# A two-layer graph network with an expert-choice FFN: gathers of 128 rows, a written order of the engines, and a + relu(b − a) on TensorE

## The chip, the cores and the metric

The program runs on one NeuronCore of a Trainium2 chip. A core has five engines with their own instruction streams: TensorE (PE, matmuls, with a separate stream of weight loads, PEld), VectorE (DVE), ScalarE (ACT), GpSimd (POOL) and SyncE (SP), and 16 DMA engines that all of them share. An engine takes its instructions strictly in the order in which they stand in its stream; engines wait for each other through semaphores. The metric is the time of one execution on the device in microseconds. Three runs of the kernel before took 1171.47, 1177.69 and 1181.61 us; the median, 1177.69 us, is what the changed kernel is compared with.

## The reference

The input is a matrix `x` of 1250 nodes with 512 features, and a list of 41,250 edges sorted by destination. All data are fp32.

```
def graph_conv_max(x, src, dst, W_rel, b, W_root):
    agg = segment_max(x[src], dst, num_segments=1250)
    agg = where(isfinite(agg), agg, 0)
    return agg @ W_rel.T + b + x @ W_root.T

h = relu(graph_conv_max(layernorm(x), ..., W1_rel, b1, W1_root))
h = relu(graph_conv_max(h,            ..., W2_rel, b2, W2_root))
x = x + h
y = layernorm(x)                       # 1250 x 512
# expert choice: 8 experts, each takes the 512 nodes with the highest probability
probs = softmax(y @ Wr, axis=0)
x = x + sum over experts of  prob * (gelu(y[chosen] @ W1 + b1) @ W2 + b2)
```

A node has 33 incoming edges on average, so a layer takes the maximum over some 41,250 rows of 2 KB.

## The kernel before

The nodes lie in ten tiles of 125 (`TN`, `NT`). The rows that may be sources stand in DRAM in `table_d`, ten blocks of 126 rows: 125 nodes and one row of −1e30. The same rows are in SBUF as `xb`. The function `fast_gnn` does the two graph layers, `expert_choice` the rest; a slower general version behind a flag is not run for these inputs. The maximum for a tile of 125 destinations is put together from three kinds of sources:

- **Blocks** (`from_blocks`, line 380 for the matmuls). For each destination tile and each of the ten source blocks, up to two sources per destination are picked by a one-hot matrix: two fp32 matmuls, (126 x 125 one-hot)ᵀ times (126 x 512 of `xb`), into the two halves of a PSUM tile `pq`. ACT first casts the one-hots from bf16 to fp32 (`ohf`, line 376), two blocks at a time. DVE takes the maximum of the whole `pq` (125 x 1024) into `acc2` (lines 386 and 388), and at the end of a tile joins the two halves. That is 200 matmuls and 90 such maxima in a layer.
- **Own gathers.** Seven more sources per destination (`K0`, indices `nat_i`) are fetched from `table_d` by indirect DMAs on POOL's queue. One such gather brings one row for each of the 125 destinations.
- **Late gathers.** What is left over is written to `rest_d` in an order sorted by how much is left (indirect DMAs, line 347), read back as dense lists `late_i`, gathered (107 gathers in a layer), and the maxima are stored to `ovf_d`. Each node fetches its row from there by its `slot_i`.

In `fetched` (line 402), up to four gathers fill one of the four buffers `hb` (pool `hist`), and DVE reduces them (lines 406 to 417). In `aggregate`, a tile whose sources are all in is transposed on PE, multiplied by `W_rel`, and added to the root part `x @ W_root + b`, which `root_part` (lines 222 to 248) has stored to `root_d` earlier. In the first layer `hidden` writes the result to `xb` and `table_d[1]`; in the second `residual` adds `x`, normalizes, stores `y_d` and transposes it into `yT`.

Ahead of the first layer stands a prefix. It finds for each node where its edges begin (`q_f`, ten gathers `row_i` at line 168, `first`), fetches each node's 64 keys (`win`, line 194), and a loop over the ten tiles (lines 259 to 298) then sorts each node's sources into blocks, own and rest: some 30 short DVE instructions for each tile (`cand`, `top`, `sel`, `new`, `ov`). From the block lists PE and ACT make a small tile `lt`, which goes through DRAM (`idx_d`) and comes back spread over 126 partitions as `ohs`.

Nothing in `fast_gnn` fixes the order of the instructions: a scheduler lays each engine's stream from its own estimates, and so interleaves, for instance, the DVE instructions of two tiles, or puts all ten root parts of the second layer (PE, 525 to 580 us) ahead of its blocks.

Of the kernel before, what the change touches and what calls it, by code (L numbers as in the profile page):

```python
# [20 lines left out]
NEGT = -1.0e30  # L21

def fast_gnn(tc, ctx, sh, io, y_d):
# [26 lines left out]
    keep = ctx.enter_context(tc.tile_pool(name="fkeep", bufs=1))  # L52
    key_d = dram.tile([1, NE + W], F32, name="key_d")
# [4 lines left out]
    ovf_d = dram.tile([N, D], F32, name="ovf_d")  # L58
# [15 lines left out]

    fr_i = gw.tile([1, NF], I32, name="fr_i")
# [5 lines left out]
    df, jle, key = (scratch[:, k * LE:(k + 1) * LE] for k in range(3, 6))  # L81
    nc.sync.dma_start(d_i, dst)
    nc.scalar.dma_start(s_i, src)
    pl_i = gw.tile([P, 1], I32, name="pl_i")
    nc.vector.memset(pl_i, 0)
# [3 lines left out]
    for t in range(NT):  # L89
        (nc.scalar if t % 2 else nc.sync).dma_start(acc[:TN, t, :], x[t * TN:(t + 1) * TN, :])  # L90

    node = gw.tile([P, NT], F32, name="node")
    nc.gpsimd.iota(node, pattern=[[TN, NT]], base=0, channel_multiplier=1,
                   allow_small_or_imprecise_dtypes=True)
    iota_w = gw.tile([P, W], F32, name="iota_w")
    nc.gpsimd.iota(iota_w, pattern=[[1, W]], base=0, channel_multiplier=0,
                   allow_small_or_imprecise_dtypes=True)
    iota_p = gw.tile([P, 1], F32, name="iota_p")
    nc.gpsimd.iota(iota_p, pattern=[[0, 1]], base=0, channel_multiplier=1,
                   allow_small_or_imprecise_dtypes=True)  # L100
    top_c = gw.tile([P, NB, R], F32, name="top_c")
    nc.gpsimd.iota(top_c, pattern=[[-BR, NB], [0, R]], base=C, channel_multiplier=0,
                   allow_small_or_imprecise_dtypes=True)
    none_c = gw.tile([P, NB, R], F32, name="none_c")
    nc.gpsimd.iota(none_c, pattern=[[-BR, NB], [0, R]], base=C - BN, channel_multiplier=0,
                   allow_small_or_imprecise_dtypes=True)
    bins = iota_w[:, :NBIN]
    after = gw.tile([P, TN], F32, name="after")
    nc.gpsimd.memset(after, 1.0)
    nc.gpsimd.affine_select(out=after, in_=after, compare_op=ALU.is_equal, fill=0.0, base=-1,  # L110
                            pattern=[[-1, TN]], channel_multiplier=1)
    wrap = gw.tile([P, TN], F32, name="wrap")
    nc.gpsimd.memset(wrap, 0.0)
    nc.gpsimd.memset(wrap[0:1, TN - 1:TN], 1.0)
    last = gw.tile([P, TN], F32, name="last")
    nc.gpsimd.memset(last, 0.0)
    nc.gpsimd.memset(last[:, TN - 1:TN], 1.0)
    ones_b = gw.tile([P, TN], BF16, name="ones_b")
    nc.gpsimd.memset(ones_b, 1.0)
    lower_b = gw.tile([P, TN], BF16, name="lower_b")  # L120
    nc.gpsimd.memset(lower_b, 1.0)
    nc.gpsimd.affine_select(out=lower_b, in_=lower_b, compare_op=ALU.is_gt, fill=0.0, base=0,
                            pattern=[[1, TN]], channel_multiplier=-1)
    lim = gw.tile([P, NBIN], F32, name="lim")
    nc.gpsimd.memset(lim, 1.0e9)
    for i in range(NT - 1, -1, -1):
        nc.gpsimd.memset(lim[:, CAPS[i]:CAPS[i] + 1], float(i * TN))
    negrow = gk.tile([P, D], F32, name="line", bufs=9)[0:1, :]
    nc.gpsimd.memset(negrow, NEGT)
    zerorow = gk.tile([P, D], F32, name="line", bufs=9)[0:1, :]  # L130
    nc.gpsimd.memset(zerorow, 0.0)


    fr_f = gw.tile([1, NF], F32, name="fr_f")
    nc.vector.tensor_copy(fr_f, fr_i)
    pfr = ps_m.tile([P, D], F32, name="pm")
    nc.tensor.matmul(pfr[:TN, :NF], ones_row[:, :TN], fr_f, start=True, stop=True)
    q_f = gw.tile([P, NT], F32, name="q_f")
    junk = gw.tile([P, NF], F32, name="junk")
    for t in range(NT):  # L140
        nc.vector.tensor_scalar(junk[:TN, :], pfr[:TN, :NF], node[:TN, t:t + 1], None, op0=ALU.is_lt,
                                op1=ALU.add, accum_out=q_f[:TN, t:t + 1])
    nc.vector.tensor_scalar(q_f[:TN], q_f[:TN], -1.0, 0.0, op0=ALU.add, op1=ALU.max)
    q_i = gw.tile([P, NT], I32, name="q_i")
    nc.vector.tensor_copy(q_i[:TN], q_f[:TN])

    nc.vector.tensor_copy(df, d_i)
    plf = gw.tile([P, 1], F32, name="plf")
    nc.vector.tensor_copy(plf, pl_i)
    bad = gw.tile([P, 4], F32, name="bad")  # L150
    nc.vector.scalar_tensor_tensor(jle[:, 1:], df[:, 1:], 0.0, df[:, :LE - 1],
                                   op0=ALU.add, op1=ALU.is_lt, accum_out=bad[:, 0:1])
    nc.vector.tensor_tensor(bad[:, 1:2], df[:, 0:1], plf, op=ALU.is_lt)
    nreal = gw.tile([P, 1], F32, name="nreal")
    nc.vector.tensor_scalar(jle, df, float(N) - 0.5, None, op0=ALU.is_lt, op1=ALU.add, accum_out=nreal)


    nc.vector.tensor_single_scalar(b_i, s_i, 1049, op=ALU.mult)
    nc.vector.tensor_single_scalar(b_i, b_i, 17, op=ALU.logical_shift_right)
    nc.vector.tensor_tensor(key, s_i, b_i, op=ALU.add)  # L160
    nc.vector.tensor_scalar(key, key, -1.0, float(C), op0=ALU.mult, op1=ALU.add)
    nc.sync.dma_start(key_d[:, :NE].rearrange("o (p j) -> (o p) j", j=LE), key)
    nc.sync.dma_start(key_d[:, NE:], zerorow[:, :W])

    cnt = gw.tile([P, NT], F32, name="cnt")
    for t in range(NT):
        row_i = gk.tile([P, FRW], I32, name="row_i", bufs=2)
        nc.gpsimd.indirect_dma_start(
            out=row_i[:TN, :], out_offset=None, in_=dst_q,
            in_offset=bass.IndirectOffsetOnAxis(ap=q_i[:TN, t:t + 1], axis=0))  # L170
        row = gk.tile([P, FRW], F32, name="row", bufs=2)
        nc.scalar.copy(row[:TN], row_i[:TN])
        nc.vector.tensor_scalar(junk[:TN, :FRW], row[:TN], node[:TN, t:t + 1], None, op0=ALU.is_lt,
                                op1=ALU.add, accum_out=cnt[:TN, t:t + 1])
    first = gw.tile([P, NT], F32, name="first")
    nc.vector.scalar_tensor_tensor(first[:TN], q_f[:TN], float(FRW), cnt[:TN], op0=ALU.mult, op1=ALU.add)
    first_i = gw.tile([P, NT], I32, name="first_i")
    nc.vector.tensor_copy(first_i[:TN], first[:TN])
    pnx = ps_m.tile([P, D], F32, name="pm")
    nc.tensor.matmul(pnx[:TN, :NT], after[:TN, :], first[:TN, :], start=True, stop=False)  # L180
    nc.tensor.matmul(pnx[:TN, :NT - 1], wrap[:TN, :], first[:TN, 1:NT], start=False, stop=False)
    nc.tensor.matmul(pnx[:TN, NT - 1:NT], last, nreal, start=False, stop=True)
    deg = gw.tile([P, NT], F32, name="deg")
    nc.vector.tensor_sub(deg[:TN], pnx[:TN, :NT], first[:TN])
    pad = gw.tile([P, NT], F32, name="pad")
    nc.vector.tensor_scalar(pad[:TN], deg[:TN], 0.5, float(C), op0=ALU.is_lt, op1=ALU.add)
    over = gw.tile([P, NT], F32, name="over")
    nc.vector.tensor_single_scalar(over[:TN], deg[:TN], W + 0.5, op=ALU.is_gt)
    nc.vector.reduce_sum(bad[:TN, 2:3], over[:TN], axis=AX.X)

    wins = []
    for t in range(NT):
# [26 lines left out]
    def transposed(rows, dest):  # L219
        pt = ps_t.tile([P, KC, P], F32, name="pt")  # L220
        for c in range(KC):
            nc.tensor.transpose(pt[:, c, :TN], rows[:, c * P:(c + 1) * P], ident[:TN, :TN])
# [113 lines left out]
    for k in (2, 3):  # L336
        nc.vector.tensor_add(bads[:TN], bads[:TN], bad[:TN, k:k + 1])
# [840 lines left out]
```

## Time and profile before

The profiled execution took 1169.04 us, of which the profile shows a span of 1167.3 us.

| engine | busy us | share of the span |
|---|---|---|
| PE | 812.3 | 70% |
| DVE | 632.3 | 54% |
| POOL | 637.7 | 55% |
| ACT | 170.3 | 15% |

No engine is busy all the time, and the share that one has differs from stage to stage. The stages can be read off from when certain tiles are first and last touched:

| us | stage |
|---|---|
| 0 to 58 | loads of `x`, search for the edges; the first `win` lands at 59 |
| 58 to 215 | lists, first root parts, first own gathers and blocks, `rest_d` |
| 215 to 405 | first layer, late gathers beside blocks |
| 405 to 525 | first layer, own gathers, matmuls with `W_rel`, `table_d[1]` |
| 525 to 583 | second layer, root parts |
| 583 to 875 | second layer, gathers beside blocks |
| 875 to 936 | last tiles of the second layer one after the other, until `y` is complete |
| 936 to 1167 | expert choice |

The trace writes two records for each fp32 matmul, so the 400 matmuls of line 380 are x800 in its groups. The granted clock of PE is 1.00 where PE is busy without a break and down to 0.50 where it is mostly idle.

### The profile page before, as it was taken

Reading aid. Unit: us, or ns where it says so; the run is one execution under the profiler, and the core shown is the slowest. Engines: PE = TensorE matmul, PEld = TensorE weight load, DVE = VectorE, ACT = ScalarE, POOL = GpSimd, SP = SyncE. Lnnn points to the kernel's source line nnn. Section 1 sums busy time; section 2 is a strip of 40 time slices with the busy share of each in tenths; the row PEclk is TensorE's granted clock in tenths of the full one; section 3 lists DMA queues with packets and bytes.
Section 4 is the critical chain, followed back from the end, with each engine's and each line's share of the span. In section 5 each row is a group of like instructions: output and inputs, shape, how many; then the busy total and the mean of one; then the engine's idle time right before and its main releaser. Section 6 shows DMA issues by size and latency. Waiting matters only on the chain.

```text
span 1167.3 us, 7551 instructions
## 1 busy us (share of the span) xinstructions
PE 812.3 (70%) x1967; PEld 351.3 (30%) x1967; DVE 632.3 (54%) x1343; ACT 170.3 (15%) x317; POOL 637.7 (55%) x512
## 2 busy tenths in 40 slices
PE   2097069453876749899987676599755652699994
PEld 1032023111322214344433222243323331344442
DVE  5271488454876639531387766498753257622321
ACT  1111011000111101122211111011111110122220
POOL 2435303688888368845588888778850000245652
PEclk9999579756898879899998988799887865699998
DMA  4226741356555465655545666746651220467874
GB/s 139 77 88 180 173 154 32 99 157 165 162 166 167 135 193 154 176 162 177 153 145 158 175 175 166 217 125 176 177 160 57 69 82 0 160 151 174 192 142 65
DMA packets 121477, 165.55 MB, mean 142 GB/s; under 512 B 65692, under 2 KB 70172, under 8 KB 121426
## 3 DMA queue, kind: packets, MB, share of 16 engines
q0 software_dynamic: 92704, 114.40, 38.3%
q1 hardware_dynamic: 27640, 49.12, 13.3%
q10 hardware_dynamic: 1082, 1.47, 0.4%
q8 instruction: 18, 0.29, 0.1%
q14 instruction: 33, 0.27, 0.1%
HBM read 135.03 MB, written 29.45 MB: 141 GB/s over the span
## 4 chain that ended last, share of the span: by engine, by line
DMA 28%; PE 25%; POOL 17%; DVE 16%; issue 11%; ACT 1%; SPq 0%; ACTq 0%; DVEq 0%; POOLq 0%
POOL hb L402 16%; DMA hb<-table_d,late_i 9%; PE pq L380 6%; DMA hb<-table_d,nat_i 6%; PE pm L1041 5%; PE pm L1048 4%; DVE acc L388 4%; DMA hb<-ovf_d,slot_i 3%; PE pm L244 3%; DMA line<-in_x 2%; DMA row_i<-in_dst,q_i 2%; DMA acc<-in_x 1%; DMA table_d<-xb 1%; PE pt L1035 1%; DVE jk L944 1%
## 5 line engine op out<-in xcount | busy, mean ns | idle before, releaser
L380 PE MATMUL pq<-xb,ohf 126*125 126x512 f32 x800 | 419.4, 674 | 161.9 <-DVE acc L388 82.2
L402 POOL DMA_INDIRECT hb<-table_d,late_i x214 | 292.5, 1367 | 105.5 <-issue 76.4
L380 PEld LDWEIGHTS pq<-xb,ohf 126*125 126x125 f32 x800 | 159.8, 211 | 407.1 <-issue 194.0
L402 POOL DMA_INDIRECT hb<-table_d,nat_i x140 | 195.3, 1395 | 76.7 <-issue 34.7
L406 DVE TENSOR_TENSOR hb<-hb 125x1024 f32<-125x1024 f32 x83 | 101.4, 1222 | 244.5 <-DMA hb<-table_d,late_i 124.4
L388 DVE TENSOR_TENSOR acc<-acc,pq 125x1024 f32<-125x1024 f32 x160 | 194.5, 1215 | 40.1 <-PE pq L380 39.8
L376 ACT CAST ohf<-ohs 126x500 f32<-126x500 bf16 x100 | 60.7, 609 | 399.7 <-PE pq L380 393.2
L1021 POOL DMA_INDIRECT ysel<-y_d,idx x32 | 30.9, 967 | 110.7 <-DVE oh L1005 73.0
L244 PE MATMUL pm<-wroot,turn 128*125 128x512 f32 x160 | 75.1, 613 | 1.1 <-ACT turn L223 1.1
L457 PE MATMUL pm<-wrel,turn 128*125 128x512 f32 x160 | 75.7, 609 | 0.0
L1052 POOL DMA_INDIRECT out<-oo,idx x32 | 50.4, 1574 | 28.7 <-DVE oo L1051 19.9
L1041 PE MATMUL pm<-yselT,w 128*128 128x512 f32 x128 | 58.0, 607 | 1.2 <-ACT yselT L1036 0.9
L1048 PE MATMUL pm<-w,hT 128*128 128x512 f32 x128 | 57.7, 599 | 0.0
L1051 DVE TENSOR_SCALAR oo<-pm,val 128x512 f32<-128x512 f32 x32 | 24.0, 751 | 59.6 <-PE pm L1048 59.6
L416 DVE TENSOR_TENSOR hb<-hb 125x512 f32<-125x512 f32 x73 | 49.9, 685 | 1.4 <-DMA hb<-table_d,late_i 1.1
L347 POOL DMA_INDIRECT rest_d<-rest,slot_i x10 | 11.9, 1189 | 63.5 <-DVE flag_i L340 60.8
L457 PEld LDWEIGHTS pm<-wrel,turn 128*125 128x125 f32 x160 | 30.8, 197 | 44.5 <-issue 35.3
L244 PEld LDWEIGHTS pm<-wroot,turn 128*125 128x125 f32 x160 | 29.4, 191 | 42.8 <-issue 38.5
L402 POOL DMA_INDIRECT hb<-ovf_d,slot_i x20 | 25.4, 1269 | 25.3 <-DMA line<-root_d 18.9
L385 ACT COPY acc<-pq 125x1024 f32<-125x1024 f32 x20 | 20.2, 1012 | 111.4 <-DVE acc L390 55.9
L859 POOL MEMSET alike<- 128x128 f32 x1 | 0.2, 204 | 64.2 <-PE pm L457 64.2
L417 DVE TENSOR_TENSOR acc<-acc,hb 125x512 f32<-125x512 f32 x40 | 27.4, 685 | 12.2 <-DMA hb<-ovf_d,slot_i 11.9
(226 smaller groups left out, 718.3 us busy)
## 6 DMA issues: line engine op xcount, KB each, us to landing
w<-in_fw SPq DMA_DIRECT2D x16, 512.0 KB
ohs<-idx_d SPq DMA_DIRECT2D x10, 615.2 KB
table_d<-xb SPq DMA_DIRECT2D x20, 250.0 KB
root_d<-line SPq DMA_DIRECT2D x20, 250.0 KB
ovf_d<-line SPq DMA_DIRECT2D x20, 250.0 KB
line<-root_d SPq DMA_DIRECT2D x20, 250.0 KB
hb<-table_d,late_i POOLq DMA_INDIRECT x214, 5.9
line<-in_x SPq DMA_DIRECT2D x10, 250.0 KB
```

Source lines behind the costliest of these rows:

```text
L244: nc.tensor.matmul(pm[:TN], hT[:, c, :], wr[:, c, :], start=(c == 0), stop=False)
L376: nc.scalar.copy(ohf[:BR].rearrange("p k n -> p (k n)"), ohs[:BR, t, b * R * TN:(b + 2) * R * TN])
L380: nc.tensor.matmul(pq[:TN, r, :], ohf[:BR, (b % 2) * R + r, :], xb[:BR, b, :], start=True, stop=True)
L388: nc.vector.tensor_max(acc2[:TN], acc2[:TN], pq[:TN])
L402: nc.gpsimd.indirect_dma_start(out=hb[:TN, k, :], out_offset=None, in_=table[:, :], in_offset=bass.IndirectOffsetOnAxis(ap=idx, axis=0))
L406: nc.vector.tensor_max(hb[:TN, 0:2, :], hb[:TN, 0:2, :], hb[:TN, 2:4, :])
L416: nc.vector.tensor_max(hb[:TN, 0, :], hb[:TN, 0, :], hb[:TN, 1, :])
L457: nc.tensor.matmul(pm[:TN], agT[:, c, :], weights[layer][2][:, c, :], start=False, stop=(c == KC - 1))
L1021: nc.gpsimd.indirect_dma_start(out=ysel[:, c, :], out_offset=None, in_=y_d[:, :], in_offset=bass.IndirectOffsetOnAxis(ap=idx[:, c:c + 1], ...
L1041: nc.tensor.matmul(ph[:, :CAP], w1[:, k, f * P:(f + 1) * P], yselT[:, k, :], start=(k == 0), stop=(k == KC - 1))
L1048: nc.tensor.matmul(po, hT[:, f, c * P:(c + 1) * P], w2[:, f, :], start=(f == 0), stop=(f == FC - 1))
L1052: add = nc.gpsimd.indirect_dma_start(out=out[:, :], out_offset=bass.IndirectOffsetOnAxis(ap=idx[:, c:c + 1], axis=0), in_=oo[:, :], in_off ...
```

## The change

All edits are in `fast_gnn`; `expert_choice` is as it was.

1. **Written order.** Calls on DVE, ACT, PE and POOL go through a wrapper that tells the scheduler to keep them in the order of the program. DMAs on SP's and ACT's queues are not wrapped.
2. **128 rows.** All gathers into SBUF take 128 indices and write 128 partitions; the three extra indices are zero. Stores of 125 rows to `table_d`, `ovf_d` (now called `late_d`) and `y_d` are split into 112 and 13 rows, and `x` is loaded by six DMAs, three tiles at a time, split likewise. Loads of `root_d`, `x` and `rest_d` rows, and stores to `root_d`, keep their 125.
3. **a + relu(b − a).** The second one-hot of a block has the first subtracted from it (`onehots`). A block is now three fp32 matmuls: the difference into a tile `pd`, Relu by ACT into `up`, then the first source and an identity times `up`, both accumulated into half of `pq`. Two blocks share one `pq`, so DVE takes one 125 x 1024 maximum for two blocks. The difference of the next block stands on PE ahead of the two matmuls of the present one.
4. **Order of the work.** The ten searches gather into one buffer without waiting for each other; normalization is batched; root parts of the first layer stand after the search and in the list loop; four tiles (`EARLY`) make their own gathers early, with their maxima merged in the list loop and after it; four pairs of blocks (`AHEAD`) run before the late lists. Then `aggregate` spreads the block pairs evenly over the groups of four gathers, with the remaining one-hots (first layer) or root parts (second layer) between them. After the last group, a tile's matmuls with `W_rel` (`conv`) are written ahead of the maxima of the next tile. In the second layer `conv` ends in `residual`, which now leaves the last steps of a tile to the next call (`finished`).

```diff
+    def __getattr__(self, name):                 # class InOrder
+        call = getattr(self.engine, name)
+        def pinned(*args, **kwargs):
+            made = call(*args, **kwargs)
+            self.tc.keep_in_program_order(made)
+            return made
+        return pinned
...
+    dve, act, pe, pool = (InOrder(tc, e) for e in (nc.vector, nc.scalar, nc.tensor, nc.gpsimd))
...
+    def stored(dest, rows):
+        for p0, p1 in SPLIT:                     # ((0, 112), (112, TN))
+            nc.sync.dma_start(dest[p0:p1, :], rows[p0:p1])
...
+    def onehots(t):
+        ob = ohs[:BR, t, :]
+        dve.tensor_scalar(ob, ob, iota_p[:BR], None, op0=ALU.is_equal)
+        pair = ob.rearrange("p (b r n) -> p b r n", r=R, n=TN)
+        dve.tensor_sub(pair[:, :, 1, :], pair[:, :, 1, :], pair[:, :, 0, :])
...
+    def gathers(rows):
+        hb = hp.tile([P, G * D], F32, name="hb").rearrange("p (g d) -> p g d", g=G)
+        for k, (table, idx) in enumerate(rows):
+            pool.indirect_dma_start(
+                out=hb[:, k, :], out_offset=None, in_=table[:, :],
+                in_offset=bass.IndirectOffsetOnAxis(ap=idx, axis=0))
+        return hb, len(rows)
...
+    for t in range(NT):
+        listed(t)
+        if t < NT - half:
+            root_part(0, half + t)
+        if t < EARLY:
+            early.append([gathers(rows) for rows in grouped(own(0, t))])
+        if t in (5, 6):
+            onehots(t - 5)
+        if t in (6, 8):
+            e = (t - 6) // 2
+            for k, hb_g in enumerate(early[e]):
+                merged(hb_g, acc[:TN, e, :], k == 0)
...
-            pq = ps_q.tile([P, 2, D], F32, name="pq")
-            for r in range(R):
-                nc.tensor.matmul(pq[:TN, r, :], ohf[:BR, (b % 2) * R + r, :], xb[:BR, b, :],
-                                 start=True, stop=True)
...
-                nc.vector.tensor_max(acc2[:TN], acc2[:TN], pq[:TN])
...
+        def begun(t, b):
+            if b % 2 == 0:
+                ohf = gk.tile([P, 2 * R, TN], F32, name="ohf", bufs=3)
+                act.copy(ohf[:BR].rearrange("p k n -> p (k n)"),
+                         ohs[:BR, t, b * R * TN:(b + 2) * R * TN])
+            pd = ps_m.tile([P, D], F32, name="pm")
+            pe.matmul(pd[:TN], ohf[:BR, (b % 2) * R + 1, :], xb[:BR, b, :], start=True, stop=True)
+            up = gk.tile([P, D], F32, name="up", bufs=3)
+            act.activation(up[:TN], pd[:TN], AF.Relu)
+            ups[t, b] = (up, ohf)
+        def ended(t, b):
+            up, oh = ups.pop((t, b))
+            if b % 2 == 0:
+                pqs[t] = ps_q.tile([P, 2, D], F32, name="pq")
+            pq = pqs[t]
+            pe.matmul(pq[:TN, b % 2, :], oh[:BR, (b % 2) * R, :], xb[:BR, b, :], start=True, stop=False)
+            pe.matmul(pq[:TN, b % 2, :], ident[:TN, :TN], up[:TN], start=False, stop=True)
+            return pq
+        begun(*work[0])
+        for n, (t, b) in enumerate(work):
+            if n + 1 < len(work):
+                begun(*work[n + 1])
+            pq = ended(t, b)
+            if b % 2 == 0:
+                continue
+            if b == 1:
+                acc2 = gk.tile([P, 2, D], F32, name="acc2", bufs=1)
+                act.copy(acc2[:TN], pq[:TN])
+            else:
+                dve.tensor_max(acc2[:TN], acc2[:TN], pq[:TN])
...
+    def aggregate(layer, blocks, done, groups, finish, beside):
+        for n, (rows, into, fresh, store) in enumerate(groups):
+            hb_g = gathers(rows)
+            due = (n + 1) * NT * NB // 2 // len(groups)
+            while done < due:
+                next(blocks)
+                done += 1
+            if n % 3 == 2 and beside:
+                beside.pop(0)()
...
+                merged(hb_g, ao[:TN], fresh)
...
+        order = list(range(EARLY, NT))
+        for t in range(EARLY):
+            order.insert(2 * t + 1, t)
+        waiting = None
+        for t in order:
...
+            fetched = [gathers(rows) for rows in grouped((own(layer, t) if t >= EARLY else []) + back(t))]
+            if waiting:
+                conv(layer, *waiting, finish)
+            for hb_g in fetched:
+                merged(hb_g, acc[:TN, t, :], False)
+            waiting = (t, rl, xt)
+        conv(layer, *waiting, finish)
...
+    def residual(t, pm, xt):
+        finished()
+        dve.scalar_tensor_tensor(acc[:TN, t, :], pm[:TN], 0.0, xt[:TN], op0=ALU.max, op1=ALU.add)
+        moments(t)
+        spread(t, t + 1)
+        unfinished.append(t)
```

`merged` holds the same DVE maxima as `fetched` did, `listed` the list loop's body, `own` and `back` the index columns of the own gathers and of the one gather from `late_d`; `turned` is the transposition on PE with its copy by ACT, `moments`, `spread` and `normed` the parts of the normalization.

## Prediction

> **What bounds the kernel now.** I read the chain first, to see which engines the end hangs on, then the costliest groups, then each engine's busy time by stage.
>
> ```profile
> DMA 28%; PE 25%; POOL 17%; DVE 16%; issue 11%; ACT 1%; SPq 0%; ACTq 0%; DVEq 0%; POOLq 0%
> ...
> L380 PE MATMUL pq<-xb,ohf 126*125 126x512 f32 x800 | 419.4, 674 | 161.9 <-DVE acc L388 82.2
> L402 POOL DMA_INDIRECT hb<-table_d,late_i x214 | 292.5, 1367 | 105.5 <-issue 76.4
> ...
> L406 DVE TENSOR_TENSOR hb<-hb 125x1024 f32<-125x1024 f32 x83 | 101.4, 1222 | 244.5 <-DMA hb<-table_d,late_i 124.4
> L388 DVE TENSOR_TENSOR acc<-acc,pq 125x1024 f32<-125x1024 f32 x160 | 194.5, 1215 | 40.1 <-PE pq L380 39.8
> ```
>
> The chain is spread over four engines. PE waits for DVE to empty `pq` (82 us), DVE for late gathers (124 us), POOL mostly for its own issue. So the gather stages are a ring. By stage (start and length, busy PE, PEld, DVE, ACT, POOL, then clock, DMA share, GB/s):
>
> ```profile
> 215.00:405.00 190.00, 122.54 (x217) 44.53 (x216) 121.03 (x152) 20.37 (x31) 145.92 (x107) 0.78 0.57 158
> ...
> 525.00:583.00 58.00, 58.00 (x158) 24.24 (x157) 11.24 (x13) 13.36 (x24) 31.07 (x24) 1.00 0.56 163
> 583.00:725.00 142.00, 103.80 (x202) 39.69 (x201) 102.70 (x112) 20.31 (x31) 116.44 (x84) 0.88 0.58 164
> ...
> 875.00:930.00 55.00, 34.59 (x89) 18.03 (x90) 15.19 (x34) 6.78 (x15) 0.00 (x0) 0.78 0.22 66
> ```
>
> From 215 to 405 and 583 to 725 POOL is busiest (77 and 82%), and PE's clock is 0.78 and 0.88. From 525 PE runs without a break at 1.00. A gather of 125 rows takes 1.21 us and 0.30 us to the next (POOL at 216.46); the 128-row gathers of the expert stage take 0.95 and 0.30 (at 1010.26): 1.51 against 1.25.
>
> **The change, part by part,** in the profiled execution's time (span 1167.3, whole 1169.04).
>
> *Price of a block.* At 580 us, 18 records of line 380 take 7.99 us; less the last one's modelled 0.59 that is 7.40/17 = 0.435 a record, 0.87 us a matmul at full clock. Six for a pair of blocks are 5.22; I take 5.3. 100 pairs cost PE 530 us, where 400 matmuls took 348: 182 us more work on PE. DVE loses 90 of 180 maxima of 1.22 us (110 us). ACT gains 200 Relus of 0.60 (as at line 462), 120 us; per pair 1.2 plus a cast of 0.61, far below 5.2. POOL: 107 gathers x 1.25 = 134 us a layer against 162. So in the block stages the bound passes to PE, at 1.00, as in the row at 525.
>
> *Prefix.* Before, `q_f` is done at 25.7 and `first` at 55.5, the searches waiting in turn for two buffers. Now `q_i` stands ahead of the checks, at some 12; ten searches x 1.25 and a landing of 4 put `first` at 29. The list loop then begins on DVE at 36.7. A list's 30 dependent short instructions took 4.0 us when two tiles were interleaved (line 295 starts at 64.10 and 68.10). In the written order each waits for the one before: a dependent start follows after duration + 0.04, where an independent one follows 0.13 after the last, which gives 6.4. Ten lists are 64; PE's five root parts hold the third up by 6; one-hots 3, two early merges 8, slots 6: end at 124.5 (before 190.9). Ten puts x 1.49 = 15, landing and read 5, until 144.4; DVE is in the maxima of the first blocks until 146.5, then the first dense list takes 2.7: the first late gather at **149** instead of 214.9. Bounds for a list are 4.0 and 6.4: I take the upper, because nothing stands between the dependent ones; the lower gives 14 us less, after the 6 of the wait and 4 of PE are taken off.
>
> *First blocks.* Four `AHEAD` pairs run on PE from 122 to 145. Then pair 6 waits until the DVE has merged the first late groups (about 166). Pair 8 ends at 178. Here PE loses some 11 us.
>
> *Rest of the first layer's blocks.* 42 pairs x 5.3 = 223, until **401** (before 405). What was won ahead is spent here: PE has more to do.
>
> *First layer's convolutions.* Before 405 to 525, 120 us, with two blocks' worth of matmuls a tile still in it. Now only gathers: last store lands 8 us on (`732.38 7.78`, the row of `ovf_d`), 45 gathers x 1.25 = 56, 7 for `root_d` loads in the same DMA engines, landing 4, merge 2.6, last `conv` 6.6: **84**, until 485. The term of 7 is one such load's time (7.18 at 882.30 in the chain), as if it landed late once; it lies between 0 and that. I take the upper end: these loads keep 125 rows, and the DMA share is only 0.24 at 71 GB/s in the stretch from 890 to 900 us, where such loads move alone. The Trainium skill, "DMA: Bandwidth & Descriptors", section "Why a DMA increments its semaphore by 16 and not by 1", says that a transfer uses the largest number of engines up to 16 that divides its rows: 5 for 125, 16 for 112. The row at 890 agrees (0.24 is below 5/16 = 0.31).
>
> *Second layer's blocks.* 50 x 5.3 = 265, ten root parts of 6.0 (58 us for ten, at 525) = 60, no longer in front but between pairs, and 4 of bubbles: 329, until **814** (before 875).
>
> *Second layer's convolutions.* Here the saving goes. `conv` of tile t−1 is written ahead of the merges of tile t, and `residual` is in `conv`: DVE must wait for PE's matmuls before it may merge the next tile, and PE for that merge. In the first layer `hidden` is on ACT, so it does not. From the rows of before: transposition at 882.98 to last matmul 889.50 is 6.5 us at a clock of 0.83 (5.05 at 1.00, at 520 us), DVE's part after it 1.85. Six steps of 8.45 = 51, four of 7.1 = 28, merges 5 x 5.2 + 4 x 0.7 = 29, first tile 14, ends 3: **125**, until 939. Before, tiles 1 to 6 overlapped blocks, and only the last ones, 875 to 936, were one after the other (row 875: DVE 15 of 55 us, POOL nothing). Full clock would give 9 less.
>
> *Tail.* Untouched: 231.4. Sum 939 − 0.2 + 231.4 = **1170**, with the 1.7 around it 1171.9. The profiled run was 1169.04 where the median is 1177.69, a factor of 1.0074: **1181**.
>
> *Costed at nothing.* Split stores: issues of 0.33 us on SP, which has little else; but root stores of tiles 0 to 4 stand on SP ahead of half the table stores, and if late delay the first own gathers: up to 9 us by a landing of 13 (`82.66 13.27`), twice. The subtraction in `onehots` (bf16, 125 x 1250) between 0.43 and 2.0 us by line 998 (640 ns for 400 columns), I take 0.7; six of ten are hidden under PE. The 128-row gathers could stay at 1.51: +12.
>
> One rule speaks against it. In the row at 580 to 590 us PE is busy 9.82 of 10 us at clock 1.00, while `pq` goes round two buffers; by that row the clock costs nothing. The Trainium skill, "TensorE: Matmul & The Clock Gate", section "A second HAM failure mode: psum-queue depth-cycling", says that cycling of PSUM buffers makes short pauses in which the clock falls back. Estimate by the rule, with the clock of row 583 (0.88): 488/0.88 − 488 = +67 us. I go by the row.
>
> ```profile
> 580.00:590.00 10.00, 9.82 (x24) 3.97 (x23) 8.84 (x10) 1.80 (x3) 6.82 (x5) 1.00 0.66 189
> 620.00:630.00 10.00, 4.95 (x8) 1.40 (x6) 4.90 (x6) 1.52 (x2) 8.31 (x6) 0.83 0.52 156
> ```
>
> The second row shows the opposite: where PE waits for half of the time, the clock is 0.83.
>
> **Rivals.** *The ends are cheaper than my rows.* For: the list at 4.0 (−14), `conv` at 1.00 (−9), no collision in the first layer's convolutions (−7), 5.22 per pair at most −8. Against: the dependent gaps, and the clock of 0.78 at 875. All would be −38; most likely some two thirds, −33 with overlap of the last blocks and merges: 1148.
>
> *PE waits for ACT* (slower). Every second block a cast (0.61) stands on ACT behind a Relu that waits for PE. The next difference needs the cast, and while it is written PE has two matmuls (1.74) against Relu 0.60 + cast 0.61 + hand-overs of about 0.25 each: about 0.03 of slack. If 0.3 us a pair is lost, 92 pairs lose 28; at 0.6, 55: 1209 to 1236. It decides from a hand-over of some 0.3. For: row 620, the clock falls once PE waits, which feeds itself. Against: three `ohf` buffers, and PE's weight loads run beside matmuls (L380 PEld 211 ns).
>
> *The change does not do what it says:* PE's clock stays at 0.9 in the block stages, because of the merges' waits for gathers: 488/0.9 − 488 = +54, 1235.
>
> **How the numbers follow.** The forecast of 1181 (PE bound, serial chain) 0.40, own range 1165 to 1200; ends cheaper 0.28; ACT 0.25; clock 0.07. A measurement here can tell about 1% from no change: 1166 and 1189. Of the forecast 0.24 lies within, 0.02 below, 0.14 above; the cheap case's 0.28 is below; of the ACT case 0.02, with a small loss, lies within and 0.23 above; the clock case is above. That gives 0.30, 0.26 and 0.44. For the range, the cheap case to −38 and a few us of bubbles (1138), and the ACT case to 55 (1240, which covers the clock case): 0.15 is left out.
>
> **What would show it.** Right: PE 9 tenths or more with clock near full from about 180 to 400 and 485 to 815; gathers of 0.95 us; first late gather about 150; in the last 120 us ahead of the expert stage DVE waiting for PE's `pm` in steps of about 13 us a tile, PE clock about 0.8; expert stage 231. Wrong: lists of 4 us; PE idle before differences with ACT's `ohf` as releaser (a pair of 5.6 or more); PE waiting for DVE's `pq` or `acc2`; late gathers still 1.2 us; tiles in the last stage overlapping.

## The result, and the profile after

The changed kernel took 1234.76 us (median of four runs, 1224.73 to 1242.66) against 1178.58 us for the kernel before, which had a fourth run by then: a ratio of 1.048, 95% interval 1.039 to 1.057. It is slower by 56 us, where the forecast had 1181 and the range ended at 1240. The profiled execution has a span of 1231.3 us at a mean clock of 0.887.

In the changed kernel the instructions of DVE, ACT, PE and POOL are recorded at the line of the wrapper, so every row has L34, and one tells them apart by tiles. These groups answer to the ones shown of the kernel before (busy time, mean ns, idle time ahead and what ended most of it):

```profile
L34 POOL DMA_INDIRECT hb<-table_d,late_i x214 | 216.9, 1014 | 272.8 <-DVE line L34 191.0
L34 DVE TENSOR_TENSOR acc<-acc,pq 125x1024 f32<-125x1024 f32 x80 | 97.7, 1221 | 298.8 <-PE pq L34 254.1
...
L34 PE MATMUL pm<-xb,ohf 126*125 126x512 f32 x400 | 209.1, 605 | 11.7 <-ACT ohf L34 7.4
L34 PE MATMUL pq<-xb,ohf 126*125 126x512 f32 x400 | 206.9, 599 | 12.0 <-DVE acc L34 12.0
L34 PE MATMUL pq<-up,ident 125*125 125x512 f32 x400 | 206.8, 598 | 0.0
```

The main waits have turned round. Before, PE waited 134 us for DVE to empty `pq`, at two lines, of which the prediction counts only the first (us in total, times, longest):

```profile
PE pq L380 <- DVE acc L388: 82.2, 32, 10.7
PE pq L380 <- DVE acc L386: 51.9, 10, 8.1
```

Now PE waits 12 us, and DVE waits 254 us for PE. Before, POOL waited mostly for its own issue; now it waits 191 us for DVE, which releases the gather buffers. The stages (start and end, length, busy PE, PEld, DVE, ACT, POOL, then clock, DMA share, GB/s):

```profile
0.00:161.00 161.00, 74.30 (x164) 30.47 (x165) 99.83 (x480) 15.61 (x35) 51.72 (x85) 0.78 0.54 163
161.00:186.00 25.00, 25.00 (x60) 10.60 (x59) 18.09 (x39) 9.44 (x17) 13.92 (x10) 0.98 0.10 19
186.00:441.00 255.00, 237.20 (x542) 101.64 (x540) 130.76 (x178) 83.49 (x143) 115.97 (x114) 0.97 0.48 128
441.00:527.00 86.00, 55.83 (x140) 24.36 (x140) 34.75 (x42) 11.78 (x21) 48.32 (x45) 0.82 0.63 194
527.00:856.00 329.00, 315.00 (x740) 134.06 (x740) 132.21 (x146) 104.91 (x179) 143.22 (x142) 0.98 0.47 133
856.00:987.00 131.00, 68.98 (x176) 33.11 (x176) 59.11 (x103) 12.97 (x29) 46.64 (x45) 0.77 0.49 147
```

In the two block stages (third and fifth row) PE is busy 93 and 96% of the time at a clock of 0.97 and 0.98, and POOL is below half. From 856 to 987 no engine is busy for more than 53%: that is a chain. And the first row is long: 161 us until the slots are known.

Set against the marks of the forecast (us from the start of the span):

| mark | forecast | measured | its own stage, forecast and measured |
|---|---|---|---|
| first late gather | 149 | 186.3 | 149, 186 |
| first layer's blocks end | 401 | 439.5 | 252, 253 |
| first layer ends | 485 | 526.5 | 84, 87 |
| second layer's blocks end | 814 | 856 | 329, 330 |
| product with the router's weights runs without a break | 939 | 990.6 | 125, 135 |
| end of the span | 1170 | 1231.3 | 231, 241 |

Of the 61 us that are missing, 37 lie ahead of the first late gather. DVE's order there (start, length, instruction, and in brackets the idle time before it and what ended it):

```profile
35.59 0.16 DVE L34 TENSOR_REDUCE bad<-over 125x1 f32<-125x10 f32 x1
69.32 0.19 DVE L34 RECIPROCAL rstd<-rstd 125x5 f32<-125x5 f32 x1 [33.57 <-ACT rstd L34]
69.54 2.37 DVE L34 TENSOR_SCALAR xb<-acc,mvs,rstd 125x512 f32<-125x512 f32 x5
71.82 0.29 DVE L34 SCALAR_TENSOR_TENSOR keys<-iota_w,deg,win 125x64 f32<-125x64 f32 x1
```

DVE has nothing to do for 33.57 us, and the lists begin at 71.82. It waits for one square root on ACT, which ACT does here:

```profile
61.48 0.57 ACT L34 COPY turn<-pt 128x500 f32<-128x500 f32 x1
68.59 0.58 ACT L34 COPY line<-pm 125x512 f32<-125x512 f32 x1 [6.53 <-PE pm L34]
69.08 0.21 ACT L34 ACTIVATE rstd<-rstd 125x5 f32<-125x5 f32 x1
```

Its operand was ready at 35.2. But in the program `spread(half, NT)` stands behind the root parts of tiles 0 to 4, ACT copies twice for each of them, and each copy waits for PE. In a pinned order a root of 0.21 us so waits for 33 us of matmuls that it doesn't need.

### The profile page after: what moved, and what is told of

Read it like the earlier page. It is cut to its first block, busy times and chain, and to the rows that moved or that the text cites. A ratio compares the mean times of both kernels' runs of the same rounds, so it can differ in the third digit from the quotient of the medians.

```text
span 1231.3 us, 8347 instructions
## 1 busy us (share of the span) xinstructions
PE 948.6 (77%) x2367; PEld 422.8 (34%) x2367; DVE 566.7 (46%) x1252; ACT 275.1 (22%) x499; POOL 503.6 (41%) x516
## 3 DMA queue, kind: packets, MB, share of 16 engines
q0 software_dynamic: 38368, 116.29, 35.8%
## 5 line engine op out<-in xcount | busy, mean ns | idle before, releaser
L34 POOL DMA_INDIRECT hb<-table_d,late_i x214 | 216.9, 1014 | 272.8 <-DVE line L34 191.0
L34 DVE TENSOR_TENSOR acc<-acc,pq 125x1024 f32<-125x1024 f32 x80 | 97.7, 1221 | 298.8 <-PE pq L34 254.1
L34 POOL DMA_INDIRECT hb<-table_d,nat_i x140 | 143.6, 1026 | 196.5 <-DVE acc L34 64.7
L34 PE MATMUL pm<-xb,ohf 126*125 126x512 f32 x400 | 209.1, 605 | 11.7 <-ACT ohf L34 7.4
L34 PE MATMUL pq<-xb,ohf 126*125 126x512 f32 x400 | 206.9, 599 | 12.0 <-DVE acc L34 12.0
L34 PE MATMUL pq<-up,ident 125*125 125x512 f32 x400 | 206.8, 598 | 0.0
L34 ACT ACTIVATE up<-pm 125x512 f32<-125x512 f32 x200 | 119.3, 597 | 311.3 <-PE pm L34 247.2
L34 DVE TENSOR_TENSOR hb<-hb 125x512 f32<-125x512 f32 (+2 forms) x161 | 152.4, 946 | 77.6 <-DMA hb<-table_d,nat_i 43.7
L34 PEld LDWEIGHTS pm<-xb,ohf 126*125 126x125 f32 x400 | 74.1, 189 | 115.1 <-issue 64.7
L34 PEld LDWEIGHTS pq<-xb,ohf 126*125 126x125 f32 x400 | 75.1, 188 | 111.2 <-issue 93.5
L34 PEld LDWEIGHTS pq<-up,ident 125*125 125x125 f32 x400 | 76.1, 190 | 98.4 <-issue 94.3
L34 PE MATMUL pm<-wroot,turn 128*125 128x512 f32 x160 | 86.4, 690 | 18.7 <-ACT turn L34 15.4
L34 PE MATMUL pm<-wrel,turn 128*125 128x512 f32 x160 | 85.4, 682 | 13.8 <-issue 13.6
L34 PE MATMUL pt<-ident,acc 125*128 125x125 f32 x80 | 15.4, 326 | 76.4 <-DVE rstd L34 40.9
L34 ACT CAST ohf<-ohs 126x500 f32<-126x500 bf16 x100 | 60.0, 600 | 0.0
L34 PEld LDWEIGHTS pm<-wrel,turn 128*125 128x125 f32 x160 | 34.9, 225 | 67.8 <-issue 57.4
L34 PEld LDWEIGHTS pm<-wroot,turn 128*125 128x125 f32 x160 | 32.9, 216 | 60.7 <-issue 40.7
```

The source lines that it names most:

```text
L34: made = call(*args, **kwargs)
```

## The experiments

Theory at this point: (A) the slow-down against the forecast comes from places where a pinned order puts a waiting instruction ahead of ready work, the square root on ACT and the merges of the last stage on DVE; and, under it, three matmuls a block make PE the bound of the block stages, so that the gain of the 128-row gathers isn't seen. Rivals: (B) transfers set the prefix and the last stage; (C) PE waits for ACT; (D) the written order as such costs or saves the time. Kernels of one comparison ran on one chip beside the kernel before, whose medians were 1179.37 (first four), 1173.38 (second four) and 1174.06 (last four); ratios are taken within a comparison.

### The square root first

```diff
-    for t in range(half):
-        root_part(0, t)
     for t in range(half, NT):
         moments(t)
     spread(half, NT)
+    for t in range(half):
+        root_part(0, t)
```

> Edit: the moments and the square root of tiles 5 to 9 are written ahead of the root parts of tiles 0 to 4. DVE's order is unchanged; on ACT the root (0.21 us) stands ahead of ten copies instead of behind them. Theory A (a wait in ACT's queue holds DVE from 35.75 to 69.32): DVE goes on at about 37, the lists begin at about 39 instead of 71.8. The third list then waits for PE to take its list out of one of the two loc buffers, behind the five root parts that end at 68.6: 69 - 57 = about 12 us of the 33 are lost again. Late gathers 21 us earlier, time 1214. Theory B (the prefix waits for transfers: x, win, table): the lists begin where they did, time unchanged, 1235.

Measured: 1218.32 us, ratio 1.032 (1.023 to 1.041). The lists begin at 37.8 instead of 71.8, and the first late gather comes at 164.3, 22 us earlier. Then the third list stops, as expected, at its subtraction:

```profile
67.69 0.18 DVE L34 TENSOR_TENSOR loc<-top_c,sel 125x20 f32<-125x20 f32 x1 [11.41 <-issue]
```

PE's row of the same moment, a transposition behind the root parts, is what it waited for: PE takes the first list out of its buffer only then.

```profile
66.33 1.12 PE L34 MATMUL pm<-brow,ones_row 1*125 1x512 f32 x2
67.38 0.28 PE L34 MATMUL pt<-ident,loc 125*20 125x125 f32 x1
```

So the wait on ACT is shown to be the one that held DVE, and theory B falls for the prefix: at 37.8 the first `win` was there, 34 us before the changed kernel used it.

### The root parts in the list loop

```diff
     for t in range(half, NT):
         moments(t)
     spread(half, NT)
-    (root parts of 0 to 4 ahead of them)
...
         listed(t)
-        if t < NT - half:
-            root_part(0, half + t)
+        root_part(0, t)
```

> Edit: as the one before, and the root parts of tiles 0 to 9 stand one behind each list in the list loop. Theory A: the whole wait goes, lists from about 39, one root part of 6 to 7 us beside one list of 6.45, so PE ends the loop some 5 us behind DVE: first late gather at about 155 instead of 186, time 1204. Theory B: 1235. If PE's root parts hold the lists: between, 1215 to 1225.

Measured: 1206.51 us, ratio 1.028 (1.020 to 1.035), 28 us less than the changed kernel; first late gather at 157.9. The place where the forecast went wrong is worth 28 us of time.

### The merges of tile t ahead of the matmuls of tile t−1

```diff
-            if waiting:
-                conv(layer, *waiting, finish)
             for hb_g in fetched:
                 merged(hb_g, acc[:TN, t, :], False)
+            if waiting:
+                conv(layer, *waiting, finish)
```

> Edit: in the last stage of a layer the maxima of tile t are written ahead of the matmuls of tile t-1 instead of behind them. Theory A (a serial chain: merges wait for the residual of the tile before, its matmuls for its merges): the second layer's last stage, 130 us from the last block maximum at 857 to the last normalization at 987, becomes bound by PE (10 x 7.5 = 75 us) and POOL (45 x 1.25 = 56 and landings): about 90 us, time 1195. The first layer's stage, with its result on ACT, stays within 5 us. Theory B (gathers and the loads of x set the steps of 9 and 14 us): at most 10 us less, 1225 or more.

Measured: 1204.84 us, ratio 1.024 (1.017 to 1.031). In the last stage of the second layer DVE waited in the changed kernel (total, times, longest, us):

```profile
DVE acc L34 <- PE pm L34: 55.0, 9, 6.6
DVE hb L34 <- DMA hb<-ovf_d,slot_i: 8.4, 1, 8.4
```

and with the merges first:

```profile
DVE acc L34 <- PE pm L34: 13.5, 4, 3.6
DVE hb L34 <- DMA hb<-ovf_d,slot_i: 8.3, 1, 8.3
```

The stage, from the last block matmul to the last store of `y_d`, is 96 us instead of 132. That the chain of merges, matmuls and residual set it is shown; loads and gathers, which are the same in both, are not what set it.

### No pinned order

```diff
-            self.tc.keep_in_program_order(made)
```

> Edit: the wrapper no longer pins the order; the scheduler lays the streams of DVE, ACT, PE and POOL from the same program. Theory A (the loss against the forecast sits in two places where a written order puts a wait ahead of ready work): the scheduler moves the square root forward and mixes the lists of two tiles, 40 to 60 us less in the prefix, and part of the last stage, 1180. Theory B (the written order is what keeps PE without a break in the block stages): PE's clock falls below 0.95 there, time 1235 to 1290.

Measured: 1221.23 us, ratio 1.038 (1.028 to 1.047), 14 us less than the changed kernel. The first late gather comes at 166.2, and from the last block matmul to the last store of `y_d` it is 64 us instead of 132, but the blocks themselves last until 912 instead of 856. Both theories were half right: the scheduler avoids most of the two waits, and its block stages are longer, at a clock of 0.90 and 0.93. Why they are longer is not shown: besides its order, this profile has the most of the unexplained stretches that the last section tells of (ACT waits 75 us in all in them). So the written order as such (D) shows no large cost and no large gain here, within that uncertainty.

### Two matmuls a block in the changed kernel

```diff
-            pe.matmul(pd[:TN], ohf[:BR, (b % 2) * R + 1, :], ...)      # and Relu, base, identity
+            pq = ps_q.tile([P, 2, D], F32, name="pq")
+            for r in range(R):
+                pe.matmul(pq[:TN, r, :], ohf[:BR, (b % 2) * R + r, :], xb[:BR, b, :], start=True, stop=True)
...
+                dve.tensor_max(acc2[:TN], acc2[:TN], pq[:TN])       # for each block
```

(The subtraction in `onehots` is out too.)

> Edit: part 3 undone inside the changed kernel: the one-hots are not subtracted, a block is two matmuls into the two halves of pq and one maximum of 125 x 1024 on DVE; order, gathers and everything else stay. Theory A (PE bounds the block stages, 5.15 us a pair): a pair costs PE 3.44 us; DVE then has 50 x 2.44 and some 90 of merges a layer, 212 us beside POOL's 134 to 170, so the first layer's stage loses some 15 to 40 us and the second's 330 us some 60 to 90: time 1155 (1120 to 1165 at most 1175). Theory B (without the third matmul the ring of before is back: PE waits for DVE to empty two pq, its clock falls to 0.8, and the written order adds waits): 1210 or more.

Measured: 1140.36 us, ratio 0.973 (0.967 to 0.978). That is 94 us below the changed kernel (15 to 30 of them uncertain, for a reason told at the end), though DVE takes 180 such maxima again instead of 80. Theory A holds, and it is the largest single effect in the changed kernel.

### Roots, merges and two matmuls together

> Edit: roots in the list loop, maxima of tile t ahead of the matmuls of tile t-1, and two matmuls a block, together. If the three gains are of different stages they add: 28 and 30 us as measured, and what the run with two matmuls alone gives (80 by theory A): 1097. If theory B of that run holds: 1175 to 1180.

Measured: 1071.72 us, ratio 0.914 (0.909 to 0.919): faster than both kernels, and 10 us below what the single gains add up to (1082).

### Roots and merges with three matmuls

> Edit: the changed kernel with three matmuls a block, with the two places mended that cost it most against the forecast: roots in the list loop, and maxima of tile t ahead of the matmuls of tile t-1. Theory A (they lie in different stages and add, 28 + 30 us): 1177, no difference from before. Theory B (time won ahead is lost in a later wait): 1195 or more.

Measured: 1133.63 us, ratio 0.966 (0.962 to 0.970). More than expected: both places mended make the kernel with all four parts faster than the one before. By the single runs 1177 was expected. By the profiles the surplus of 43 us lies in the prefix (10), the first layer (15) and the second layer's blocks (17), and none of it in the last stage. Those are the stages in which the changed kernel and the two single runs have the stretches told at the end, and this run has none; that they are the whole of it is not shown. What is left is PE: the chain of this kernel reads

```profile
PE 65%; DMA 9%; DVE 6%; POOL 4%; issue 3%; ACT 2%; SPq 0%; POOLq 0%; DVEq 0%; ACTq 0%
```

The same kernel with two matmuls is the run above: 62 us less, with the same order and the same gathers. Its second layer's block stage, and that of this kernel:

```profile
445.00:733.00 288.00, 244.03 (x540) 98.92 (x540) 191.00 (x195) 47.63 (x80) 142.57 (x142) 0.95 0.53 152
```

```profile
475.00:795.00 320.00, 311.67 (x740) 133.08 (x740) 132.14 (x145) 105.54 (x181) 142.77 (x142) 1.00 0.48 137
```

200 more matmul records cost 68 us of PE, and 32 us of the stage; DVE's 59 us less buy nothing, since it isn't the bound in either.

### The 128-row gathers alone, in the kernel before

```diff
-                    out=hb[:TN, k, :], ... IndirectOffsetOnAxis(ap=idx)      # 125 indices
+                    out=hb[:, k, :], ...                                     # 128, three of them zero
-            nc.sync.dma_start(ovf_d[i * TN:(i + 1) * TN, :], ao[:TN])        # likewise table_d, y_d
+            for p0, p1 in ((0, 112), (112, TN)):
+                nc.sync.dma_start(ovf_d[i * TN + p0:i * TN + p1, :], ao[p0:p1])
```

(The searches and the key windows take 128 rows here too.)

> Edit: part 2 alone in the kernel before: gathers of 128 rows, and split stores of table_d, ovf_d and y_d (the loads of x stay). 374 gathers and 20 searches at 1.25 instead of 1.51 us take 100 us off POOL. Theory A (POOL and its landings are part of the ring from 215 to 405 and 583 to 875): a third of it shows, 1145. Theory B (the ring is set by pq and DVE, the gathers are covered): within 10 us, 1170 to 1180.

Measured: 1078.13 us, ratio 0.921 (0.916 to 0.926). Three times what theory A expected: 95 us. With the stores left whole (gathers alone):

> Edit: the kernel before with all gathers into SBUF of 128 rows, but the stores of 125 rows whole. Theory A (the 95 us of part 2 come from the gathers: 1.25 instead of 1.51 us on POOL, landings of 4.1 instead of 5.9 us): 1080 to 1095. Theory B (the split stores give a good part, since late rows are stored to be gathered again): 1110 or more.

Measured: 1090.23 us, ratio 0.928 (0.923 to 0.934). So the gathers give 84 us. The split stores give some 8 more by the ratios (a difference of 0.007), which the overlapping intervals do not show; in the two profiles all of it lies ahead of the first late gather, which comes at 186 us with them and at 200 without. The late gathers, before (min, median and max ns of the instruction and of the landing, first and last start):

```profile
L402 POOL DMA_INDIRECT hb<-table_d,late_i x214: 1207/1212/3169, 214.9 to 722.4; - x107
...
DMA to landing us min/median/max: 4.9/5.9/9.4
```

and with 128 rows and split stores:

```profile
L408 POOL DMA_INDIRECT hb<-table_d,late_i x214: 942/947/3168, 186.2 to 646.0; - x107
...
DMA to landing us min/median/max: 3.4/4.1/8.6
```

From the slots to the end of the first layer it is 298 us instead of 333, and the second layer's blocks take 299 instead of 326. 107 gathers x 0.265 = 28 us a layer would explain most of that, if POOL's issue sets the pace of the ring in the kernel before. That is argued from the size: no run separates the shorter issue from the landings, which are 1.8 us shorter.

### Three matmuls alone, in the kernel before

```diff
+                nc.tensor.matmul(pd[:TN], ohf[:BR, (b % 2) * R + 1, :], xb[:BR, b, :], start=True, stop=True)
+                nc.scalar.activation(up[:TN], pd[:TN], AF.Relu)
+                (base and identity into half of pq, one maximum for two blocks)
```

> Edit: part 3 alone in the kernel before, in the scheduler's own order. PE gets 182 us more of matmuls, DVE 110 less. Theory A (PE bounds the block stages as soon as a block has three matmuls): the first layer's stage of 190 us, with 68 of idle PE, and the second's of 292, with 73, take up at most two thirds of it: 1230 (1215 to 1260). Theory B (DVE's relief pays for it): 1180 or less.

Measured: 1399.61 us, ratio 1.192 (1.185 to 1.199). The direction was theory A's, the size not: 226 us, more than the 182 us of added matmuls. Some waits of this kernel, PE's and DVE's:

```profile
PE pq L386 <- DVE acc L394: 145.8, 36, 9.0
...
PE pq L388 <- ACT up L383: 24.7, 10, 10.5
```

```profile
DVE hb L412 <- DMA hb<-table_d,late_i: 229.1, 45, 65.0
DVE hb L412 <- DMA hb<-table_d,nat_i: 156.7, 19, 28.8
```

and a piece of its PE timeline:

```profile
263.12 1.02 PE L381 MATMUL pm<-xb,ohf 126*125 126x512 f32 x2
268.16 2.07 PE L386 MATMUL pq<-xb,ohf 126*125 126x512 f32 x2 [4.02 <-DVE acc L394]
270.02 1.91 PE L388 MATMUL pq<-up,ident 125*125 125x512 f32 x2
271.73 1.91 PE L381 MATMUL pm<-xb,ohf 126*125 126x512 f32 x2
```

PE still waits for DVE, which stands in a merge and waits for its gather (229 us in all, 124 before); after such waits pairs of records take up to 1.91 instead of 1.02 us. So in this kernel the ring stands with three matmuls too, and the added work of PE doesn't go under its waits.

### 125-row gathers in the changed kernel

```diff
-                out=hb[:, k, :], ...          # 128 indices
+                out=hb[:TN, k, :], ...        # 125 indices
```

> Edit: the changed kernel with the gathers of table_d and late_d rows back at 125 rows (searches and key windows stay at 128). Theory A (PE bounds the block stages, so the gathers are covered there and show only in the two last stages of the layers, 45 gathers each, and at the first groups): 0.26 x 90 = 23 and some of the landings: 1260 (1245 to 1275). Theory B (the gathers are worth as much here as in the kernel before): 1320 or more.

Measured: 1223.83 us, ratio 1.044 (1.040 to 1.048), not to be told from the changed kernel's 1.048. Theory B falls: most of the 84 us that the gathers are worth in the kernel before is hidden here. Theory A's 23 us are not settled. Where it put the loss, the profiles have one: the first layer's last stage takes 97 us against 87, with POOL busy for 58 us of it instead of 48, and the second layer's 137 against 135. But this run has none of the stretches told at the end, and is quicker for it where the changed kernel has them: the first late gather comes at 177.8 instead of 186.3, and the second layer's blocks take 320 us instead of 329.

### Loads and stores of 125 rows split too

```diff
-            nc.sync.dma_start(rl[:TN], root_d[layer][t * TN:(t + 1) * TN, :])   # likewise root_d's stores, x
+            for p0, p1 in ((0, 112), (112, TN)):
+                nc.sync.dma_start(rl[p0:p1], root_d[layer][t * TN + p0:t * TN + p1, :])
```

(On top of roots, merges and two matmuls.)

> Edit: on the version with roots in the loop, maxima first and two matmuls a block, also the stores and loads of root_d and the loads of x in the second layer are split into 112 and 13 rows. Theory A (transfers of 125 rows land late because they lie on few of the 16 DMA engines): their landings fall, some 10 us less in the two last stages, 1062. Theory B (they are covered by PE and POOL): within 4 us of 1072.

Measured: 1065.44 us, ratio 0.907 (0.903 to 0.911), against 0.914 (0.909 to 0.919) without it. The two intervals overlap; a gain of some 7 us is likely and not shown. By the two profiles 6 us of it lie ahead of the first late gather and 4 in the second layer's last stage, while the first layer's last stage is 2 us longer; theory A had put all of it in the two last stages. It is the fastest version that was run.

## Why the prediction was right and where it was wrong

Right, by its own steps. *The price of a block* and the passing of the bound to PE: records of 0.43 us, 5.15 us a pair (5.22 worked out, 5.3 taken), PE 20.00 of 20 us busy at 1.00 in the stretch from 340 to 360; the two stages came out at 253 and 330 us for 252 and 329. The second of these fits in part by chance: some 9 us of it are stretches that the last section tells of (320 us without them), and the forecast had allowed 0.15 us too much a pair and 4 us of bubbles. *The first layer's last stage* at 87 for 84. *The serial chain* of the second layer's last stage, 135 for 125, without which the result can't be understood: steps of 9 us for a tile with one gather and 14 for one with eight, as priced. *The gathers* of 0.95 us, and that little hangs on them once PE is the bound (it priced their staying at 1.51 at 12 us).

Wrong: *the step "Prefix"*, and in it the sentence that the list loop begins on DVE at 36.7. It was reckoned from DVE's and POOL's queues. The move of the root parts ahead of the square root was seen only for PE (6 us at the third list); the ten copies that the root parts put on ACT's queue, two each, and the square root behind them, were left out. The wait measured 33.57 us. The run with the root parts in the list loop shows what the step was worth: 28 us. As the lists came later, the 6 us at the third list didn't arise. Another 8 us of the prefix are gaps in the third list that the last section tells of.

*Costed too low:* the last stage by 10 us, of which 3 are the router's weights (the rest is not traced): their load stands on SP behind the last stores of `y_d` (988.17), where before it was issued at 930.90, ahead of the last tile's. The tail by 10: some 7 of them between the first transposition of chosen rows and the end, 159.6 us here and 152.1 before. The nine other versions of the changed kernel have 154.7 to 159.6 there and the three of the kernel before 151.3 to 155.9, with the same lines in all; how much of it is scatter and how much the change is open.

The rival *PE waits for ACT* gave a figure (1209 to 1236) that holds the result, by another mechanism: PE waited 7.4 us in all for `ohf`, 6.3 of them at one place (568.8), where ACT stood still as the last section tells. In the steady stretch the cast ends while PE is at work, and the slack of 0.03 us that was worked out is not used up:

```profile
302.12 0.60 ACT L34 ACTIVATE up<-pm 125x512 f32<-125x512 f32 x1 [2.04 <-issue]
302.61 0.60 ACT L34 CAST ohf<-ohs 126x500 f32<-126x500 bf16 x1
304.63 0.60 ACT L34 ACTIVATE up<-pm 125x512 f32<-125x512 f32 x1 [1.43 <-PE pm L34]
```

So it is by luck that the result lies inside the stated range: the upper end of 1240 was reckoned from the 55 us of this rival, which did not come, and the range of the forecast's own mechanism ended at 1200.

The pauses that the Trainium skill describes for PSUM buffers used in turn ("TensorE: Matmul & The Clock Gate", "A second HAM failure mode: psum-queue depth-cycling", there with bf16 matmuls) did not show here. With two `pq` and the `pd` tiles in turn the clock was 1.00 from 240 to 440 us and from 587 to 847, and PE was busy without a break from 240 to 420. The measurement decides for the row.

Four readings of the prediction were off, and little hung on them: PE's wait for `pq` (134 us, not 82), the maxima that DVE is spared (100 of 180, not 90), the terms of the list loop (they add up to 123.7, not 124.5), and the load of 7.18 us, which is one of `x` and not of `root_d`.

What the prediction did not ask is what each part is worth alone. There are a gain of 95 us (128 rows, in the kernel before) and a loss of 62 us (three matmuls, in the mended order; 94 in the order as written, the unexplained stretches included), with an order that costs 69 us by two misplaced waits (1140.36 against 1071.72, both with two matmuls). What the written order is worth with these waits mended hardly shows: with two matmuls it takes 1071.72 us, and the kernel before with part 2 alone 1078.13 in the same comparison, with overlapping intervals. In the changed kernel PE sets the pace and covers most of the gathers' gain. Whether that is due to the third matmul or to the written order is not separated: the third matmul alone, in the kernel before, left the ring standing, and two matmuls in the written order were not run with 125-row gathers.

## What to carry to other kernels

When an order is written out by hand, follow each small instruction on its own engine's queue: a square root of 0.21 us behind ten copies that wait for PE cost 28 us, and merges behind a residual 30. Before trading work of one engine for another's, find which resource sets the pace: in the kernel before, cheaper gathers (0.26 us each on POOL, and earlier landings) were worth 84 us, and in the changed kernel, with its third matmul for each block, PE sets the pace and hides most of that. Measure parts of a joint change one by one; they may be of opposite sign.

## What was not expected

- **Three more rows make a gather cheaper.** 125 rows take 1.21 us of POOL's time and land after 5.9 us, 128 rows 0.95 and 4.1. The packets of POOL's queue fall from 92,704 for 114 MB to 38,368 for 116 MB in the whole program, and those under 512 B, over all queues, from 65,692 to 11,551 with the gathers alone. Why 125 rows go in small packets no run here shows.
- **Stretches in which ACT and DVE stand still with no cause in the profile.** In the profiles of the changed kernel and of the four kernels of the first comparison, and in none of the others, waits end by "remote", which stands in the row where an engine or a DMA of this core is named otherwise. On DVE and on ACT, in the second layer's blocks of the changed kernel:

```profile
564.80 1.22 DVE L34 TENSOR_TENSOR acc<-acc,pq 125x1024 f32<-125x1024 f32 x1 [8.00 <-remote]
```

```profile
567.66 0.60 ACT L34 ACTIVATE up<-pm 125x512 f32<-125x512 f32 x1 [7.21 <-remote]
```

The third list of the changed kernel loses 8 us in gaps of the same kind (2.4 of them end by "remote", the others follow DVE's own instructions), and its second layer's blocks take 329 us against 320 with 125-row gathers. Both times POOL issues gathers one behind the other, but the same gathers stop nothing in the later runs. What it is stays open. It makes comparisons of the changed kernel and the first four runs with the others uncertain, by 17 us if these two places are added. An estimate from the later runs alone gives more: the kernel with roots and merges mended has a ratio of 0.966, and mending them was worth 0.059 with two matmuls (0.973 against 0.914); if it is worth the same with three, the changed kernel without such stretches would have 1.025 instead of 1.048, 27 us less (and the 125-row gathers, at 1.044, would cost it the 23 us of theory A after all). So a part of the slow-down of 56 us may be theirs, and whether the change or the occasion brought them is open. The three causes above don't rest on it: the two waits are seen to shorten in their own stages, and the third matmul's 62 us come from two runs without such stretches.
